# Layer 1's feature products scaled on ScalarE, comparisons for four groups at once, and another order of the first transfers, in a four-layer graph network

## The chip, the cores and the metric

The kernel runs on one core of a Trainium2 chip. A core has five engines that run their own instruction streams in order: TensorE (PE; weight loads are shown apart as PEld) multiplies matrices into PSUM, VectorE (DVE) and ScalarE (ACT) work elementwise, GpSimd (POOL) here mostly issues indirect transfers (gathers and scatters by index), and SyncE (SP) issues plain transfers. ScalarE issues some transfers as well. The metric is the device time of one launch in microseconds: the median over runs, here 4229.58 us (3 runs, 4228.15 to 4233.15).

## The reference

3125 nodes with 256 features each, 50000 edges sorted by their destination, 16 edge types, 64 features per edge. Four layers, each a graph part and a mixture or feed-forward part. Only the first half of the computation matters here, layers 0 and 1:

```python
# layer 0, graph part: a matrix for each of 16 edge types
transformed = jnp.einsum('ni,rio->rno', layernorm(x), weight)
x = x + segment_sum(transformed[rel_type, src] * norm, dst)
# layer 0, mixture of 8 experts, two of them per node
x = x + moe(layernorm(x))
# layer 1, graph part: messages from an embedding table, weighted by edge features
cut = 0.5 * (cos(edge_weight * pi / CUTOFF) + 1.0) * (edge_weight < CUTOFF)
W = (edge_feats @ W_dist + b_dist) * cut[:, None]
agg = segment_sum(embed_table[node_z][src] * W, dst)
x = x + concatenate([layernorm(x), agg], 1) @ W_comb + b_comb
```

The output is x after four such layers. Everything is float32.

## The kernel before

One stage computes both layers' graph parts and layer 0's experts together (`stage_one`, L787). Ahead of it, from L378 on, the edges' fields are loaded as 125 x 400 arrays and written to DRAM as rows of a table `md` (source, type code, norm, destination, cut). x is loaded in five pieces of five node tiles each (`xs0`, L408). From each node's statistics DVE and ScalarE make the normalized rows; POOL gathers the embedding row of each node (`species`, L453); both halves together are a row of 512 numbers, and five writes (L633) put the 3150 rows into a DRAM table `tab`. A search finds where each node's edges begin: POOL fetches a row of destinations from the DRAM array `dsr` (L573), and DVE counts in it (L578). `dsr` is written by SP (L542, L543). The start of the program also has a branch for unsorted edges, which each engine passes before it comes to L541. The order of all instructions in this part and in the stage is written out by hand for each engine.

The nodes are cut into 25 tiles of 126, a tile into 21 groups of 6 nodes. The edges that end in one group lie in a window of 128 places; there are 521 windows. For a window:

- POOL gathers the 128 source rows from `tab` (`fetch_rows`, nine buffers `g`), and SP loads the transposed edge features (`fetch_feats`, six buffers `f`).
- `build` (L855), two windows ahead, makes two comparison matrices on DVE: `s0`, 128 x 96, is 1 where the edge has this node and type, times norm (L865), and `s1`, 128 x 32 (or 128 x 128 for the groups 5 and 10, which straddle two quarters of the rows), is 1 where the edge has this node, times the cut (L867).
- `window` (L873): PE multiplies the rows' normalized half with `s0` into the PSUM tile `c` (L880), which ScalarE copies to `aT` (L884), for two windows at once where they are neighbours. PE multiplies the features with `W_dist` into `pw` (L887, two PSUM banks). DVE multiplies `pw` with the rows' embedding half into `mt` (L890). After this the row buffer is free, and the gather of the window nine places on is issued.
- `add_up` (L895) multiplies `s1` with `mt` into the tile's sum `agg` in PSUM (L906), in three batches of windows.

After a tile's windows come eight slots of `weigh` (L914): 64 matmuls of `aT` with the 16 type matrices `wrel` into `f0` (L919). After the last of them DVE adds `f0` to x (L923). Each pair of tiles then starts a `Flow`: routing, experts and combination, cut into 22, 32 and 34 steps, which are laid between later windows (`between`, L1139). `between` runs once after each window and each `weigh` slot: it takes the due steps of the flows, one step of `background` (in every slot up to slot 116, then in every third), one of `late_weights` (weights on ScalarE's DMA queue) and one of `first_zeros` (zero fills of DRAM on SP's queue, 200 KB each).

`background` (L1195) prepares later layers: the searches for the other tiles, a check of windows, a product of all edge features with an attention vector (`b_at`, L1273 to L1284: 100 loads of 125 KB, two buffers, each used one step after it is issued), and a ranking of nodes by degree (L1347), where for each of 25 columns three products are accumulated: a row `base`, the columns before (`prev`) and this column.

After the last tile the remaining flow steps run one after the other. Then the stage's memory is given back, and the other layers follow, which the change does not touch.

Of the kernel before, what the change touches and what calls it, by code (L numbers as in the profile page):

```python
# [19 lines left out]
P = 128  # L20
# [75 lines left out]
def tile_gnn_ffn(ctx: ExitStack, tc: tile.TileContext, a: dict, out: bass.AP):  # L96
# [311 lines left out]
    for i in range(5):  # L408
        xg = pp.tile([P, 5, D], F32, name=f"n_x{i}")
        t = 5 * i  # L410
        m = 5 if i < 4 else 4
        if i == 4:
            nc.gpsimd.memset(xg[:, 4, :], 0.0)
            nc.sync.dma_start(xg[:TV, 4, :], a["x"][(NT - 1) * TN :, :])
        nc.sync.dma_start(xg[:TN, :m], a["x"][t * TN : (t + m) * TN, :].rearrange("(t p) d -> p t d", p=TN))
        xs0.append(xg)
        if i == 0:
            wgt = edge_in("edge_weight", F32)
            norm = edge_in("edge_weight1", F32)
# [122 lines left out]
    nc.sync.dma_start(dsr[1:, :], dstf)  # L542
    nc.sync.dma_start(dsr[:1, :], none)  # L543
# [55 lines left out]
    nc.sync.dma_start(md[:, E:].rearrange("f (p c) -> p f c", c=P), pads)  # L599

# [186 lines left out]
    def stage_one(late, cp, eb):  # L787
# [36 lines left out]
        def quarter(j):  # L824
            return None if j in (5, 10) else GN * j // 32
# [29 lines left out]
        def build():  # L855
            k = nxt["s"]
            if k < len(wins):
# [4 lines left out]
                a = quarter(j)  # L862
                a, m1 = (0, P) if a is None else (32 * a, 32)
                s1 = eb.tile([P, m1], F32, name=f"s1_{m1}", bufs=13 if m1 == 32 else 3)
                nc.vector.tensor_scalar(s0, iota_f[:, :GW], m[:, F_CODE, j : j + 1], m[:, F_NORM, j : j + 1],  # L865
                                        op0=OP.is_equal, op1=OP.mult)
                nc.vector.tensor_scalar(s1, iota_f[:, a : a + m1], m[:, F_DST, j : j + 1], m[:, F_CUT, j : j + 1],  # L867
                                        op0=OP.is_equal, op1=OP.mult)
                sums[k] = s0, s1
# [3 lines left out]
        def window(k):  # L873
# [5 lines left out]
            for h in range(2):  # L879
                nc.tensor.matmul(pc[:, h, o : o + GW], g[:, h * P : (h + 1) * P], sums[k][0], start=True, stop=True)  # L880
# [8 lines left out]
            mt = mults[t, j] = eb.tile([P, D], F32, name="mt", bufs=11), sums.pop(k)[1]  # L889
            nc.vector.tensor_tensor(mt[0], pw, rows.pop(k)[:, D:], op=OP.mult)  # L890
            fetch_rows()

        ag_of, mults = {}, {}

        def add_up(t, b):  # L895
# [4 lines left out]
            for js in together[b]:  # L900
                js = [j for j in js if (t, j) in mults]
                for j in js:
                    a = quarter(j)
                    mt, s1 = mults.pop((t, j))
                    o = agg if a is None else agg[32 * a : 32 * a + 32]
                    nc.tensor.matmul(o, s1, mt, start=not begun, stop=(j == 10), skip_group_check=True)  # L906
# [7 lines left out]
        def weigh(t, i):  # L914
# [224 lines left out]
        def between(fast=False):  # L1139
# [7 lines left out]
            next(loads, None)  # L1147
            next(zeros_, None)
# [3 lines left out]
        for _ in range(2):  # L1152
            build()
# [5 lines left out]
        for t in range(NT):  # L1159
            n = GL if t == NT - 1 else GC  # L1160
            for j in range(n):
                build()
                window(k)
                k += 1

# [15 lines left out]
            for i in range(8):  # L1181
# [3 lines left out]
                if i == 7 and (t % 2 or t == NT - 1):  # L1185
                    if t == NT - 1:
                        load_e(t // 2, 0)
                    flows.append(Flow(t // 2))
# [6 lines left out]
    def background(eb, bank):  # L1195
# [77 lines left out]
        for b in range(0, ET, AB):  # L1273
            at = eb.tile([EP, AB, 64], F32, name="b_at", bufs=2)
            nc.sync.dma_start(at, attr[:, b : b + AB, :])
            if b:
                old, b0 = prev
                nc.vector.tensor_tensor(old, old, a3[:EP].unsqueeze(1).to_broadcast([EP, AB, 64]), op=OP.mult)
                nc.vector.tensor_reduce(rect[:, b0 : b0 + AB, 1], old, axis=AX.X, op=OP.add)
            prev = at, b  # L1280
            yield
        old, b0 = prev
        nc.vector.tensor_tensor(old, old, a3[:EP].unsqueeze(1).to_broadcast([EP, AB, 64]), op=OP.mult)
        nc.vector.tensor_reduce(rect[:, b0 : b0 + AB, 1], old, axis=AX.X, op=OP.add)  # L1284
# [1256 lines left out]
```

## Time and profile before

| | |
|---|---|
| median of 3 runs | 4229.58 us |
| the profiled execution | 4229.5 us, span 4227.7 us |
| first window's matmul (L880) | 90.38 us after the span's start |
| last `weigh` matmul of the first tile | 164.4 us |
| of the last tile | 1762.6 us |
| last store of the stage issued (L1106) | 1864.6 us |
| DVE: product `mt` (L890) | 521 of 420 ns |
| DVE: comparison `s0` (L865), `s1` (L867) | 341 ns; 308 ns (32 wide), 347 ns (128 wide) |
| ScalarE: copies of `c` (L884) | 875 ns (two windows), 517 ns (one) |
| PE: products `pw` (L887) | 1042 of 445 ns |

An instruction on PE counts twice for float32: a matrix product is shown as two matmuls, each with its weight load. Matmuls overlap, so their durations do not add up to time. In the views, "idle before" or the brackets behind a line give the time that the engine stood idle before the instruction, and what ended it. Of the rest of the span, 1865 to 4228 us, nothing reads or writes what the change touches.

### The profile page before, as it was taken

The page shows a single profiled execution, that of the slowest core. Times are in us where ns is not written, and L with a number is a line of the kernel's source. Part 1 is how long each engine was busy: PE and PEld are TensorE (multiplying, and loading weights), DVE is VectorE, ACT ScalarE, POOL GpSimd, SP SyncE. Part 2 cuts the span into 40 slices and gives each one's busy share as a digit, 9 for nine tenths or more (in the row PEclk, how much of TensorE's full clock was granted, in tenths as well). Part 3 has the DMA queues.
Part 4 walks back from the last instruction along what each step waited for, and adds up shares of the span by engine and source line. Part 5 has one row for each costly group of instructions (what it writes and reads, how often), then busy time and mean ns, then how long its engine had stood idle before and what let it go on. Part 6 is the DMA issues. An engine that isn't in the chain of part 4 may idle for free. (4 is left out here: it accounts for less than half of the span.)

```text
span 4227.7 us, 46661 instructions
## 1 busy us (share of the span) xinstructions
PE 2697.7 (64%) x12940; PEld 2134.4 (50%) x12940; DVE 1946.6 (46%) x7501; ACT 845.3 (20%) x1803; POOL 1758.5 (42%) x1996
## 2 busy tenths in 40 slices
PE   1688999989889999948411365365670112137875
PEld 0566878767677878737310254254550111125653
DVE  3445666665665555442344333444662233245300
ACT  1112232221122222211100021122220000013322
POOL 4342333341253333002466544544437666643323
PEclk9878999999799999968755576577775555566987
DMA  7766455452243444113233254365523333323543
GB/s 223 223 190 187 129 157 144 130 154 65 76 118 107 118 133 126 52 48 107 73 93 91 86 175 141 107 185 168 174 90 101 87 92 88 92 81 107 158 159 100
DMA packets 275971, 521.46 MB, mean 123 GB/s; under 512 B 53609, under 2 KB 176897, under 8 KB 275685
## 3 DMA queue, kind: packets, MB, share of 16 engines
q0 software_dynamic: 105344, 306.57, 25.0%
q1 hardware_dynamic: 159598, 201.27, 15.6%
q10 hardware_dynamic: 10742, 10.34, 0.8%
q8 instruction: 114, 1.87, 0.2%
q14 instruction: 173, 1.41, 0.1%
HBM read 431.19 MB, written 86.78 MB: 123 GB/s over the span
## 5 line engine op out<-in xcount | busy, mean ns | idle before, releaser
L136 POOL DMA_INDIRECT g<-tab,m_si x521 | 498.0, 956 | 989.9 <-DVE mt L890 526.5
L136 POOL DMA_INDIRECT g_rows<-tab,srcI x413 | 401.9, 973 | 300.4 <-DVE ACC L2273 157.3
L136 POOL DMA_INDIRECT g_row<-tab,srcI x413 | 400.4, 970 | 196.3 <-issue 104.6
L880 PEld LDWEIGHTS c<-s,g 128*128 128x128 f32 x2084 | 345.8, 217 | 166.7 <-issue 83.9
L880 PE MATMUL c<-s,g 128*128 128x96 f32 x2084 | 356.1, 299 | 100.1 <-issue 38.2
L887 PE MATMUL pw<-w_d,f 65*128 65x256 f32 x1042 | 374.4, 445 | 14.2 <-DVE mt L890 11.9
L919 PE MATMUL f<-w_rel,aT 128*126 128x256 f32 x1600 | 372.6, 383 | 0.1
L884 ACT COPY aT<-c 128x384 f32<-128x384 f32 (+1 forms) x323 | 237.1, 737 | 595.7 <-PE c L880 397.5
L1982 PE MATMUL mm<-ro_xt,ro_w 128*128 128x192 f32 (+3 forms) x928 | 255.9, 428 | 122.3 <-ACT ro_h L2063 73.1
L919 PEld LDWEIGHTS f<-w_rel,aT 128*126 128x126 f32 x1600 | 300.2, 190 | 50.5 <-issue 5.3
L1651 PE MATMUL tp<-ident,ACC 128*128 128x128 f32 x50 | 16.1, 424 | 462.5 <-DVE ACC L2395 357.2
L890 DVE TENSOR_TENSOR mt<-pw,g 128x256 f32<-128x256 f32 x521 | 218.7, 420 | 159.0 <-PE pw L887 83.8
L1986 PE MATMUL y<-ro_w,ro_h 128*96 128x256 f32 (+2 forms) x1040 | 263.6, 409 | 33.5 <-ACT ro_h L2063 19.1
L1982 PEld LDWEIGHTS mm<-ro_xt,ro_w 128*128 128x128 f32 x928 | 183.8, 221 | 178.4 <-ACT ro_h L2063 80.5
L1651 PEld LDWEIGHTS tp<-ident,ACC 128*128 128x128 f32 x50 | 7.1, 199 | 470.5 <-issue 441.1
L1986 PEld LDWEIGHTS y<-ro_w,ro_h 128*96 128x96 f32 (+2 forms) x1040 | 190.4, 189 | 86.9 <-ACT ro_h L2063 23.1
L1037 PE MATMUL w<-w,b_h 128*126 128x256 f32 x800 | 218.5, 398 | 11.1 <-ACT xt L950 3.0
L1028 PE MATMUL w<-xt,w 128*128 128x252 f32 (+1 forms) x832 | 221.3, 392 | 6.3 <-issue 3.4
L140 POOL DMA_INDIRECT xg<-XX,ro_pos x100 | 101.6, 1016 | 287.6 <-issue 136.5
L2273 DVE SCALAR_TENSOR_TENSOR ACC<-g_rows,g_e,ACC 128x256 f32<-128x256 f32 x413 | 200.9, 486 | 43.9 <-DVE ACC L2273 19.9
L2395 DVE TENSOR_TENSOR ACC<-ACC,g_row 128x256 f32<-128x256 f32 x413 | 173.2, 424 | 67.1 <-DMA g_row<-tab,srcI 48.0
L2240 PE MATMUL pu<-w_s,a_xt 128*128 128x256 f32 x100 | 45.9, 606 | 231.5 <-DVE ACC L2268 104.8
(580 smaller groups left out, 4791.0 us busy)
## 6 DMA issues: line engine op xcount, KB each, us to landing
ro_w<-in_L_ffn_blocks SPq DMA_DIRECT2D x58, 514.0 KB
ro_w<-in_L_ffn_blocks SPq DMA_DIRECT2D x58, 512.0 KB
f<-in_attr_t SPq DMA_DIRECT2D x521, 32.5 KB
xg<-zero SPq DMA_DIRECT2D x78, 200.0 KB
b_at<-in_edge_attr SPq DMA_DIRECT2D x100, 125.0 KB
tabr<-v SPq DMA_DIRECT2D x12, 758.0 KB
g<-tab,m_si POOLq DMA_INDIRECT x521
g_rows<-in_L_ffn_blocks SPq DMA_DIRECT2D x14, 514.0 KB
```

Source lines behind the costliest of these rows:

```text
L136: return nc.gpsimd.indirect_dma_start(out=dst, out_offset=None, in_=table, in_offset=bass.IndirectOffsetOnAxis(ap=idx, axis=0))
L880: nc.tensor.matmul(pc[:, h, o : o + GW], g[:, h * P : (h + 1) * P], sums[k][0], start=True, stop=True)
L884: nc.scalar.copy(aT[:, :, :, b : b + n * GN].rearrange("p k r n -> p k n r"), pc[:, :, : n * GW].rearrange("p k (n r) -> p k n r", r=16))
L887: nc.tensor.matmul(pw, feats.pop(k), wd, start=True, stop=True)
L890: nc.vector.tensor_tensor(mt[0], pw, rows.pop(k)[:, D:], op=OP.mult)
L919: nc.tensor.matmul(cur["f"][:TN], aT[:, h, r, :], wrel[:, h, r, :], start=(r == 0 and h == 0), stop=(r == 15 and h == 1))
L1028: nc.tensor.matmul(ph, w["01"][:, e, k, i * P : (i + 1) * P], xt[:, k, : n * TN], start=(k == 0), stop=(k == 1))
L1037: nc.tensor.matmul(py, last[:, k, i * TN : (i + 1) * TN], w["02"][:, e - 1, k, :], start=(k == 0), stop=(k == 1))
L1982: nc.tensor.matmul(ph, w[:, o : o + P], xt[:, k, :], start=(k == 0), stop=(k == 1))
L1986: nc.tensor.matmul(py, h[:, i, s], w[:, i * D : (i + 1) * D], start=(i == 0), stop=(i == self.fc - 1))
L2273: stt(u, g[:, r, :D], e[:, r0 + r : r0 + r + 1], u, op0=OP.mult, op1=OP.add)
L2395: nc.vector.tensor_tensor(u, u, rows.pop(r), op=OP.max)
```

## The change

1. The factor `cut` moves. Before, `s1` was the comparison times `cut`. Now ScalarE reads `pw` from PSUM, multiplies by the edge's `cut` and writes `mt`, and DVE multiplies `mt` by the gathered embedding half in place.
2. The comparisons `s1` leave `build`. `whose` makes them once per batch: for the batches 0 and 1 one comparison has four groups (`s1g`, 128 x 4 x 32), two per batch; for batch 2 five single ones, without a second operation.
3. `build` runs three windows ahead instead of two.
4. The addition of `f0` to x and the start of the pair's flow move from the last `weigh` slot to the second window of the next tile (`weighed`); the last tile keeps its place.
5. Of x's five loads the first two stay at the beginning, the other three are issued by SP after the `md` writes. The two writes of `dsr` go from SP's queue to ScalarE's.
6. `late_weights` begins at slot 2 and `first_zeros` at slot 6, instead of slot 0.
7. `b_at` has three buffers and is used two steps after its issue.
8. In the ranking the row `base` is put into row 0 of `prev` once, and the separate product of one row goes.

```diff
     xs0 = []
-    for i in range(5):
+
+    def load_x0(i):
...
-        if i == 0:
-            wgt = edge_in("edge_weight", F32)
-            norm = edge_in("edge_weight1", F32)
+
+    load_x0(0)
+    wgt = edge_in("edge_weight", F32)
+    norm = edge_in("edge_weight1", F32)
+    load_x0(1)
...
-    nc.sync.dma_start(dsr[1:, :], dstf)
-    nc.sync.dma_start(dsr[:1, :], none)
+    nc.scalar.dma_start(dsr[1:, :], dstf)
+    nc.scalar.dma_start(dsr[:1, :], none)
...
     nc.sync.dma_start(md[:, E:].rearrange("f (p c) -> p f c", c=P), pads)
+    for i in range(2, 5):
+        load_x0(i)
...
-                a = quarter(j)
-                a, m1 = (0, P) if a is None else (32 * a, 32)
-                s1 = eb.tile([P, m1], F32, name=f"s1_{m1}", bufs=13 if m1 == 32 else 3)
                 nc.vector.tensor_scalar(s0, iota_f[:, :GW], m[:, F_CODE, j : j + 1], m[:, F_NORM, j : j + 1],
                                         op0=OP.is_equal, op1=OP.mult)
-                nc.vector.tensor_scalar(s1, iota_f[:, a : a + m1], m[:, F_DST, j : j + 1], m[:, F_CUT, j : j + 1],
-                                        op0=OP.is_equal, op1=OP.mult)
-                sums[k] = s0, s1
+                sums[k] = s0
...
-            mt = mults[t, j] = eb.tile([P, D], F32, name="mt", bufs=11), sums.pop(k)[1]
-            nc.vector.tensor_tensor(mt[0], pw, rows.pop(k)[:, D:], op=OP.mult)
+            del sums[k]
+            mt = mults[t, j] = eb.tile([P, D], F32, name="mt", bufs=11)
+            nc.scalar.activation(mt, pw, AF.Copy, scale=mts[t][:, F_CUT, j : j + 1])
+            nc.vector.tensor_tensor(mt, mt, rows.pop(k)[:, D:], op=OP.mult)
             fetch_rows()
...
+        def whose(t, b):
+
+            m = mts[t][:, F_DST]
+            n = GL if t == NT - 1 else GC
+            for js in together[b]:
+                js = [j for j in js if j < n]
+                if b < 2:
+                    s1 = eb.tile([P, 4, 32], F32, name="s1g", bufs=3)
+                    of = m[:, js[0] : js[-1] + 1 : 5].unsqueeze(2).to_broadcast([P, len(js), 32])
+                    nc.vector.tensor_tensor(s1[:, : len(js)], iota_f.rearrange("p (q n) -> p q n", n=32)[:, : len(js)],
+                                            of, op=OP.is_equal)
+                    for i, j in enumerate(js):
+                        ones_of[t, j] = s1[:, i, :]
+                    continue
+                for j in js:
+                    q = quarter(j)
+                    n1 = P if q is None else 32
+                    s1 = ones_of[t, j] = eb.tile([P, n1], F32, name=f"s1_{n1}", bufs=2 if q is None else 3)
+                    o = 32 * (q or 0)
+                    nc.vector.tensor_scalar(s1, iota_f[:, o : o + n1], m[:, j : j + 1], None, op0=OP.is_equal)
...
-            if i == 7:
-                x = x_of[t // 2][:TN, t % 2, :]
-                nc.vector.tensor_add(x, x, cur["f"][:TN])
+
+        def weighed(t):
+            x = x_of[t // 2][:TN, t % 2, :]
+            nc.vector.tensor_add(x, x, cur["f"][:TN])
+            if t % 2 or t == NT - 1:
+                flows.append(Flow(t // 2))
...
-            next(loads, None)
-            next(zeros_, None)
+            if slot >= 2:
+                next(loads, None)
+            if slot >= 6:
+                next(zeros_, None)
...
-        for _ in range(2):
+        for _ in range(3):
             build()
...
                 build()
+                at = wins[k][1]
+                if at in (12, 13, 5):
+                    whose(t, (12, 13, 5).index(at))
                 window(k)
                 k += 1
+                if j == 1 and t:
+                    weighed(t - 1)
...
-        for b in range(0, ET, AB):
-            at = eb.tile([EP, AB, 64], F32, name="b_at", bufs=2)
-            nc.sync.dma_start(at, attr[:, b : b + AB, :])
-            if b:
-                old, b0 = prev
+        ahead = []
+        for b in range(0, ET + 2 * AB, AB):
+            if b < ET:
+                at = eb.tile([EP, AB, 64], F32, name="b_at", bufs=3)
+                nc.sync.dma_start(at, attr[:, b : b + AB, :])
+                ahead.append((at, b))
+            if b >= 2 * AB:
+                old, b0 = ahead.pop(0)
...
+        nc.vector.tensor_copy(prev[:1, :], base[:1, :])
...
-            nc.tensor.matmul(pk, ones[:1, :], base[:1, :], start=True, stop=False)
-            nc.tensor.matmul(pk, ones, prev, start=False, stop=False)
+            nc.tensor.matmul(pk, ones, prev, start=True, stop=False)
```

More of the change, by code (lines that the diff above doesn't have):

```diff
@@ L879, in window @@
             for h in range(2):
-                nc.tensor.matmul(pc[:, h, o : o + GW], g[:, h * P : (h + 1) * P], sums[k][0], start=True, stop=True)
+                nc.tensor.matmul(pc[:, h, o : o + GW], g[:, h * P : (h + 1) * P], sums[k], start=True, stop=True)
             if second[k] or k + 1 == len(wins) or not second[k + 1]:
@@ L888, in window @@
             fetch_feats()
-            mt = mults[t, j] = eb.tile([P, D], F32, name="mt", bufs=11), sums.pop(k)[1]
-            nc.vector.tensor_tensor(mt[0], pw, rows.pop(k)[:, D:], op=OP.mult)
+            del sums[k]
+            mt = mults[t, j] = eb.tile([P, D], F32, name="mt", bufs=11)
+            nc.scalar.activation(mt, pw, AF.Copy, scale=mts[t][:, F_CUT, j : j + 1])
+            nc.vector.tensor_tensor(mt, mt, rows.pop(k)[:, D:], op=OP.mult)
             fetch_rows()
-        ag_of, mults = {}, {}
+        ag_of, mults, ones_of = {}, {}, {}
+        def whose(t, b):
[17 more added lines that the diff above has]
+                    nc.vector.tensor_scalar(s1, iota_f[:, o : o + n1], m[:, j : j + 1], None, op0=OP.is_equal)
         def add_up(t, b):
@@ L903, in add_up @@
                     a = quarter(j)
-                    mt, s1 = mults.pop((t, j))
                     o = agg if a is None else agg[32 * a : 32 * a + 32]
-                    nc.tensor.matmul(o, s1, mt, start=not begun, stop=(j == 10), skip_group_check=True)
+                    nc.tensor.matmul(o, ones_of.pop((t, j)), mults.pop((t, j)), start=not begun, stop=(j == 10),
+                                     skip_group_check=True)
                 begun = True
@@ L1184, in stage_one @@
                     add_up(t, 2)
[L1185 to L1188, printed above, removed]
+                if i == 7 and t == NT - 1:
+                    load_e(t // 2, 0)
+                    weighed(t)
                 between()
@@ L1272, in background @@
         nc.vector.tensor_copy(rect[:, :, 0], srcf)
-        for b in range(0, ET, AB):
-            at = eb.tile([EP, AB, 64], F32, name="b_at", bufs=2)
-            nc.sync.dma_start(at, attr[:, b : b + AB, :])
-            if b:
-                old, b0 = prev
+        ahead = []
[6 more added lines that the diff above has]
+                old, b0 = ahead.pop(0)
                 nc.vector.tensor_tensor(old, old, a3[:EP].unsqueeze(1).to_broadcast([EP, AB, 64]), op=OP.mult)
                 nc.vector.tensor_reduce(rect[:, b0 : b0 + AB, 1], old, axis=AX.X, op=OP.add)
-            prev = at, b
             yield
-        old, b0 = prev
-        nc.vector.tensor_tensor(old, old, a3[:EP].unsqueeze(1).to_broadcast([EP, AB, 64]), op=OP.mult)
-        nc.vector.tensor_reduce(rect[:, b0 : b0 + AB, 1], old, axis=AX.X, op=OP.add)
         nc.vector.tensor_sub(ews, ews, rect[:, :, 1])
```

## The prediction

> **What bounds the kernel now.** I read the page first: TensorE has the most work, and the digits by slice show where it is dense.
>
> ```profile
> PE 2697.7 (64%) x12940; PEld 2134.4 (50%) x12940; DVE 1946.6 (46%) x7501; ACT 845.3 (20%) x1803; POOL 1758.5 (42%) x1996
> PE   1688999989889999948411365365670112137875
> PEclk9878999999799999968755576577775555566987
> DMA  7766455452243444113233254365523333323543
> ```
>
> Each slice is 105.7 us. The change touches only layer 1's stage (slices 1 to 18); its last store is issued at 1864.6. So I cut that stage with the table by stretches, at the ends of the node tiles' last `weigh` matmuls. Columns: stretch, busy time of PE, PEld, DVE, ACT, POOL, then clock, DMA share, GB/s.
>
> ```profile
> 0.00:90.00 90.00, 2.36 (x7) 1.47 (x7) 29.72 (x135) 13.28 (x23) 34.99 (x54) 1.00 0.67 206
> 90.00:164.00 74.00, 57.23 (x236) 44.37 (x237) 32.65 (x146) 9.93 (x14) 30.16 (x32) 1.00 0.87 279
> 250.00:317.00 67.00, 60.74 (x268) 48.22 (x268) 38.05 (x152) 15.81 (x24) 25.56 (x27) 0.69 0.63 189
> 317.00:400.00 83.00, 68.06 (x309) 53.98 (x308) 45.07 (x137) 14.18 (x23) 20.82 (x22) 0.81 0.62 194
> 464.00:523.00 59.00, 57.01 (x322) 48.15 (x321) 35.54 (x129) 16.45 (x29) 21.24 (x22) 0.97 0.46 131
> 1291.00:1763.00 472.00, 451.27 (x2550) 374.53 (x2548) 250.53 (x1030) 134.67 (x250) 157.91 (x190) 0.98 0.41 115
> ```
>
> Three regimes. Up to 90 us nothing runs on PE: transfers and their order bound it. The first tile (74 us) runs at a DMA share of 0.87. A later tile takes 59 us with PE busy 97%: there PE is the bound. Between them tile 3 takes 83 us, PE 82% busy at 0.81 clock. What its DVE and PE wait for is told by the waits and the timeline:
>
> ```profile
> DVE b_at L1278 <- DMA b_at<-in_edge_attr: 36.1, 27, 3.1
> PE c L880 <- issue: 26.5, 22, 5.3
> PE c L880 <- DVE s L865: 21.8, 16, 4.1
> PE pw L887 <- DVE mt L890: 7.9, 9, 1.4
> ```
>
> (The first is of 317 to 400, the others of 317 to 1763.) And the pieces of the timeline that carry the start:
>
> ```profile
> 35.23 0.32 SPq L542 DMA_DIRECT2D dsr<-e_dstf  x1
> 39.76 0.91 POOL L136 DMA_INDIRECT q_rows<-dsr,q_rowi  x1 [16.33 <-DMA dsr<-e_dstf]
> 46.98 0.62 DVE L578 TENSOR_SCALAR_CACHE_REDUCE q_rows<-q_rows,q_node 21x400 f32<-21x400 f32 x1 [12.52 <-DMA q_rows<-dsr,q_rowi]
> 84.57 0.18 DVE L798 TENSOR_SCALAR j<-iota_f 128x21 f32<-128x21 f32 x1 [24.39 <-DMA tab<-n_row]
> ```
>
> SP issues `dsr` at 35.23 although DVE had it at 19.94: five loads of x (issued up to 26.25) and then the start's branch stand before it on SP. POOL then loses 16.33 us and DVE 12.52 us, and the table is only written at 84.5.
>
> **The change, part by part.** The sum is against the profiled 4229.5 us (span 4227.7 and 1.8 around); the median of the runs is 4229.58.
>
> *A, the start: -18 us.* Three x loads (1.9 MB) move behind SP's `md` writes, and `dsr` goes to ScalarE's queue, free at about 20 us. POOL's 16.33 us and DVE's 12.52 us go, as both were waiting for `dsr`. What is late next: statistics of tiles 10 to 14 are interleaved with the first reciprocal roots, and their x now lands after some 1 MB of writes, perhaps 3 us late; then the table. POOL's embedding gathers ended at 66.3 and would end at about 50 to 57; the table's last write then lands at 64 to 69 instead of 84.5. DMA allows it: from 30 to 45 us it moved 32 to 126 GB/s. Also the first 2 MB of `w_rel`, issued at 58.24 between the table's writes, move out to slot 2: 2.1 MB at 350 GB/s are 6 us, inside the 18. Ends: -25 (all waits and `w_rel`), -5 (x is late and only `w_rel` counts).
>
> *B, the first tile: +5 us.* That `w_rel` lands here, less six zero fills of 0.2 MB: 0.9 MB at the stretch's 279 GB/s is 3 us. ScalarE's queue is in order: the small loads behind `w_rel` held it from 93.4 to 109.8 (the `aT` copy waited 15.59 us). Now `mt` of each window stands behind them too, with the gathers that wait for it and, after two PSUM banks, PE. Ends: 0 (the DMA is full anyway) and +14 (that wait once more).
>
> *C, tiles 1 to 4: -25 us.* `b_at` gets a third buffer and is used two steps after its issue. DVE stood 51.5 us for it between 150 and 423 us; a transfer issued at 317.05 was used at 318.94, 1.9 us later, and a slot of that tile takes 2.4 or more, so two steps cover it. Behind those waits stood the x addition and `build`; PE ran dry (at 407.6 for 5.3 us, at 325.2 for 4.1) and its clock fell. Tile 3 at 62 instead of 83 gives 21, tile 4's start 5, tile 2 about 0: I take 25. Ends: -51 and 0 (the transfers are late by more under a DMA share of 0.62).
>
> *D, the later tiles: -20 us.* DVE loses 21 comparisons per tile (308 ns, two of 347) and gets 4 grouped ones (nearest row: 128x128 addition, 293 ns) and 5 single ones: 6.5 - 2.7 = 3.8 us per tile, 95 in all. It is busy 53 to 60%, so I count this only where PE waited for DVE. `mt` keeps its 420 ns; from SBUF a 128x256 product took 424. `build` runs three ahead instead of two, and the x addition no longer stands before it. Of the rows above, 56 us, some 17 are already in C; of the remaining 39 I take half. The half-rate clock that follows each such stall costs up to 70 us from 464 to 1763 (stretch times one less the clock), so the end is -80 with part of it; the other end is +36: ScalarE adds 521 products. Their row is missing; the nearest are a PSUM copy of 126x256 (372 ns) and a scaled SBUF activation (590); I take 0.42, near the copy, which also reads PSUM: 219 us on an engine busy 28% in the dense stretch. The cover is PE: of a 59 us tile 19 go to eight `weigh` slots and 40 to 21 window slots, 1.9 us each, in which ScalarE needs 0.46 for `aT` (237 us over 521), 0.42, and some 0.4 for the flows. Behind the new wait stand `aT` copies and `b_h` on ScalarE, and on DVE, after `mt`, the flows' additions; POOL's gathers run nine windows ahead and bear 1 us. If a sixth of the 0.42 reaches PE in each window, that is 0.07 x 521 = +36.
>
> The rule against this part is in the Trainium skill, ScalarE: Activation LUTs, Rules for kernel authors: products belong on VectorE rather than ScalarE. The trace says ScalarE is 20% busy and DVE 46%, so I don't follow it. By the rule, part D would bring nothing and the sum would be 20 us less gain.
>
> *E, the rank loop: -7 us.* 25 products of one row go (50 passes, 345 ns each, overlapped). In the timeline a step takes 1.06 us at full clock, of which they hold 0.42, and 0.72 at half clock; DVE itself needs 0.95 per step. So 25 x 0.1 to 25 x 0.72: 2.5 to 18. One 1-row copy is added: nothing.
>
> *F, the tail: +2 us.* A flow now starts two slots later. Covered while windows run; the last pair's two steps fall in the tail, 102 us for 88 steps. Ends 0, +4.
>
> Zero fills six slots later, and loads two, cost nothing elsewhere: 317 to 400 has DMA at 0.62, and the first `weigh` is at slot 21.
>
> One rule speaks against A: the Trainium skill, DMA: Bandwidth & Descriptors, Issuing engines are not separate DMA queues, says that another issuing engine saves only the sequencer's issue time. By it, moving `dsr` would save its two issues, 0.5 us, and A would be the 6 us of `w_rel`. The row at 35.23 is a case in which the issue itself waits, so I keep -18.
>
> Sum: -18 + 5 - 25 - 20 - 7 + 2 = -63: 4229.5 - 63 = 4166.5, say **4166 us**.
>
> **The rivals.**
> 1. *The clock recovers too.* Most half-rate time goes with the stalls: C -40, D -55, others as above: 4229.5 - 18 + 5 - 40 - 55 - 7 + 2 = 4116. For it: clock 0.69 in 250 to 317 without a long gap. Against it: searches that wait for DMA in tiles 1 and 2 stay.
> 2. *Only the start gains.* PE's gaps are filled by other waits (gathers, PSUM banks): A + B + E with its lower end + F = -18 + 5 - 2.5 + 2 = -13.5: 4216. For it: PE is already 96% busy from 1291. Against it: 36.1 us of one wait in one tile.
> 3. *ScalarE becomes the wait (slower).* Each window's `mt` stands behind an `aT` copy (875 ns per pair) and PE waits for the PSUM bank of `pw`. From 63/521 = 0.12 us of PE per window on, the gain is gone; at half of the 0.42 it costs 0.21 x 521 = 109 us in place of D's -20: -63 + 20 + 109 = +66, 4296. Against it: ScalarE waited 304 us for `c`, so it is early nearly everywhere.
> 4. *The order of transfers does nothing* (table bound by bytes): A = -6: 4178, inside the likeliest one's range.
>
> **How the numbers follow.** Likeliest, with rival 4, 60%: 4130 to 4205. Rival 1 15%. Rival 2 14%, of which 4% lies within 0.2%. Rival 3, 8%; 3% for a small loss by B and D's bad ends together. 0.2% is 8.5 us, about what a measurement of this kernel can tell from no change. Faster 0.86, same 0.04, slower 0.10. For the range I leave out the far half of rival 1 and what is slower: 4100 to 4224.
>
> **What would show it.** A: the first `c` matmul at about 72 instead of 90.4, `dsr` issued near 20. B: the first tile at 74 to 85 us. C: no `b_at` wait on DVE above 10 us in all, tile 3 near 62. D: PE's wait for `s` and for the bank of `pw` together under 20 us from 317; the scaled copies at 0.37 to 0.47. E: a rank step under 1.0 us. F: last `weigh` to last store about 104. Wrong would be: PE waiting for ScalarE in the hundreds of windows, gathers late by it, or a start still held by x or the table.

## The result: 1.05% slower where 1.5% faster was forecast

The changed kernel took 4278.0 us (median of 4 runs, 4269.8 to 4279.4), the kernel before 4231.4 us beside it: ratio 1.0105, 95% interval 1.0088 to 1.0123. The forecast was 4166 us with a range to 4224, and faster with a chance of 0.86. It was wrong in sign.

The same kernel before the change took 4216 to 4240 us in the first and the last of six sessions and 3744 to 3768 us in the four between (below: the slower and the quicker sessions), so that times are compared within a session, and across sessions only as ratios to the kernel before. The change was measured in one of each: slower by 1.05% in the first, and a gain, 0.9943 (0.9927 to 0.9959), in a quicker one. The record gives the chip number 15 to the fourth session, a quicker one, and to the last, a slower one. The texts of expectation below, written before that was known, say "the first chip" and "the later chips" for slower and quicker.

The profile after the change, of the slower kind (its execution 4278.99 us, span 4277.3). First the page's totals and slices:

```profile
PE 2702.8 (63%) x12890; PEld 2142.7 (50%) x12890; DVE 1882.7 (44%) x7205; ACT 1039.4 (24%) x2324; POOL 1768.8 (41%) x1996
...
PE   1689999988888999966612364456671112137975
...
PEclk9669999989889999987855576577775555556987
```

DVE lost 64 us of work and ScalarE got 194 us more, as the change says. PE's digits in the stage went from 9 to 8 in places: it has the same work and more gaps. Next the same stretches as before (columns as before: stretch, PE, PEld, DVE, ACT, POOL, clock, DMA share, GB/s):

```profile
0.00:90.00 90.00, 10.32 (x35) 8.51 (x35) 32.65 (x149) 15.11 (x26) 41.38 (x60) 1.00 0.64 204
90.00:164.00 74.00, 48.94 (x204) 38.31 (x204) 26.97 (x119) 16.93 (x32) 24.07 (x26) 0.77 0.87 273
317.00:400.00 83.00, 76.55 (x391) 61.59 (x389) 51.45 (x154) 28.67 (x56) 24.10 (x26) 0.92 0.69 219
1291.00:1763.00 472.00, 437.04 (x2396) 363.07 (x2395) 219.80 (x890) 177.98 (x381) 160.47 (x190) 0.95 0.39 110
```

The start is earlier (35 matmuls of PE before 90 us instead of 7), 317 to 400 does 391 matmuls instead of 309 at a clock of 0.92 instead of 0.81, and 1291 to 1763, where PE was the bound, does 2396 instead of 2550. The loss is in the late part. Cut at the ends of the tiles' `weigh` matmuls, in us of one profiled execution each, and with the forecast's terms:

| part | forecast | slower session | quicker session |
|---|---|---|---|
| A: first `c` matmul | -18 | 90.4 to 82.0: -8.3 | 89.3 to 83.4: -5.9 |
| B: from there to the first tile's end | +5 | +9.4 | +0.8 |
| C: tiles 1 to 4 | -25 | -12.5 | -16.7 |
| D and E: tiles 5 to 24 | -27 | 1299.1 to 1357.8: +58.7 | 1234.8 to 1226.2: -8.6 |
| F: from the last `weigh` matmul to the end of the span | +2 | +2.3 | +1.8 |
| sum (spans) | -63 | +49.6 | -28.6 |

So one line of the table is the error of sign: in the slower session D and E have 86 us more than forecast. What PE waited for in it, before (first fence, 463.5 to 1762.6 us) and after (second fence, 452.1 to 1809.9 us; columns: total, times, longest):

```profile
PE c L880 <- DVE s L865: 15.6, 13, 3.8
PE c L880 <- issue: 15.5, 17, 3.0
PE pw L887 <- DVE mt L890: 7.6, 8, 1.4
...
PE w L1037 <- ACT xt L950: 2.7, 5, 0.6
...
PE w L949 <- ACT xt L950: 1.9, 1, 1.9
...
PE w L1351 <- DVE k_prev L1353: 1.5, 2, 1.2
```

```profile
PE w L975 <- ACT xt L976: 19.1, 6, 6.0
PE pw L887 <- ACT mt L891: 15.0, 9, 3.0
PE pw L887 <- issue: 11.3, 6, 5.4
PE w L1382 <- DVE k_prev L1384: 10.8, 13, 3.1
...
PE w L975 <- issue: 7.1, 5, 4.1
...
PE c L880 <- DVE s L867: 5.5, 9, 1.4
```

The waits that the change was to remove did go: the rows of `c` (L880), 36.3 us with the small ones, fell to 17.5. In their place came the PSUM bank of `pw`, now released by ScalarE (26.3 us in place of 9.9), and the flows' transposes (`flip_rows`, L975; L949 before), 35.8 us in place of 2.2. All rows that name ScalarE together grew from 9.9 to 55.6 us, +45.7; PE's idle time in all grew from 82.2 to 127.4, +45.2. The time at half clock grew from 133 to 191 us. In the quicker session the same rows show almost nothing of it (changed kernel, 438.2 to 1664.4 us):

```profile
PE w L1054 <- ACT xt L976: 5.1, 10, 0.5
PE w L975 <- ACT b_h L1056: 1.5, 4, 0.4
```

There the rows that name ScalarE grew from 6.5 to 9.9 us only. PE's idle time in all rose there too, from 46.6 to 57.2 us, but the time at half clock fell from 92 to 68 us.

What differs between the sessions is seen in one flow's two transposes. The timeline of the changed kernel in the slower session, tile 23:

```profile
1709.89 0.43 PE L975 MATMUL w<-ident,xn 126*128 126x126 f32 x2
...
1711.04 0.26 PE L809 MATMUL w<-ident,m_m 105*128 105x105 f32 x1
1714.20 0.37 ACT L976 COPY xt<-w 128x252 f32<-128x252 f32 x1 [4.17 <-remote]
...
1714.62 0.43 PE L975 MATMUL w<-ident,xn 126*128 126x126 f32 x2 [3.33 <-ACT xt L976]
```

and the same instructions in the quicker session:

```profile
1573.21 0.43 PE L975 MATMUL w<-ident,xn 126*128 126x126 f32 x2
...
1573.68 0.37 ACT L976 COPY xt<-w 128x252 f32<-128x252 f32 x1 [0.61 <-PE w L975]
...
1574.37 0.26 PE L809 MATMUL w<-ident,m_m 105*128 105x105 f32 x1
...
1574.46 0.38 PE L975 MATMUL w<-ident,xn 126*128 126x126 f32 x2
```

In the quicker session ScalarE copies as soon as the transposes end, at 1573.64. In the slower one PE's records show the transposes done at 1710.3, and ScalarE, idle, starts at 1714.20, released by nothing that the profile names. The trace's semaphore events (the signals by which one engine releases another) show it: of PE's completions none is recorded from 1708.97 to 1714.07, and then seven within 0.24 us, as many as PE's instructions of that stretch signal. PE's signals came late, in a burst. Counted as a silence of over 1.5 us followed by three signals within 0.2 us, there are 33 such bursts (116 us of silence) in tiles 5 to 24 of the kernel before and 15 (72 us) in the changed one, in the slower session; in the quicker sessions' traces there is none, whatever the kernel. In the slower traces 14 to 16% of PE's signal records are missing and 23 to 25% of VectorE's, so the counts are rough; VectorE's signals, counted in the same way, show one such burst before and none after. The changed kernel lost more although it met fewer bursts, so their number does not explain its loss.

### The profile page after: what moved, and what is told of

It is laid out like the page before. It is cut to its first block, busy times and chain, and to the rows that moved or that the text cites. A ratio compares the mean times of both kernels' runs of the same rounds, so it can differ in the third digit from the quotient of the medians.

```text
span 4277.3 us, 46755 instructions
## 1 busy us (share of the span) xinstructions
PE 2702.8 (63%) x12890; PEld 2142.7 (50%) x12890; DVE 1882.7 (44%) x7205; ACT 1039.4 (24%) x2324; POOL 1768.8 (41%) x1996
## 5 line engine op out<-in xcount | busy, mean ns | idle before, releaser
L880 PEld LDWEIGHTS c<-s,g 128*128 128x128 f32 x2084 | 353.9, 220 | 100.2 <-issue 39.8
L892 DVE TENSOR_TENSOR mt<-mt,g 128x256 f32<-128x256 f32 x521 | 220.0, 422 | 405.1 <-ACT mt L891 346.6
L880 PE MATMUL c<-s,g 128*128 128x96 f32 x2084 | 356.7, 300 | 45.4 <-DMA f<-in_attr_t 21.5
L942 PE MATMUL f<-w_rel,aT 128*126 128x256 f32 x1600 | 382.5, 390 | 2.9 <-ACT aT L884 1.9
L891 ACT ACTIVATE mt<-pw,m_mt 128x256 f32<-128x256 f32 x521 | 245.6, 473 | 374.5 <-PE pw L887 232.7
L1682 PE MATMUL tp<-ident,ACC 128*128 128x128 f32 x50 | 16.3, 428 | 464.6 <-DVE ACC L2426 446.3
L1054 PE MATMUL w<-xt,w 128*128 128x252 f32 (+1 forms) x832 | 224.9, 396 | 10.5 <-ACT xt L976 6.6
L2017 PEld LDWEIGHTS y<-ro_w,ro_h 128*96 128x96 f32 (+2 forms) x1040 | 190.5, 189 | 81.4 <-issue 26.6
L1063 PE MATMUL w<-w,b_h 128*126 128x256 f32 x800 | 221.9, 404 | 7.9 <-ACT xt L976 5.3
L887 PEld LDWEIGHTS pw<-w_d,f 65*128 65x128 f32 x1042 | 183.2, 219 | 43.3 <-ACT mt L891 29.7
```

The costliest lines, as they stand in the source:

```text
L887: nc.tensor.matmul(pw, feats.pop(k), wd, start=True, stop=True)
L891: nc.scalar.activation(mt, pw, AF.Copy, scale=mts[t][:, F_CUT, j : j + 1])
L892: nc.vector.tensor_tensor(mt, mt, rows.pop(k)[:, D:], op=OP.mult)
L942: nc.tensor.matmul(cur["f"][:TN], aT[:, h, r, :], wrel[:, h, r, :], start=(r == 0 and h == 0), stop=(r == 15 and h == 1))
L1054: nc.tensor.matmul(ph, w["01"][:, e, k, i * P : (i + 1) * P], xt[:, k, : n * TN], start=(k == 0), stop=(k == 1))
L1063: nc.tensor.matmul(py, last[:, k, i * TN : (i + 1) * TN], w["02"][:, e - 1, k, :], start=(k == 0), stop=(k == 1))
```

## The experiments

**The ScalarE step.** Two edits: the changed kernel with the product and the cut in one VectorE instruction, and the kernel before with the ScalarE step alone.

```diff
-            nc.scalar.activation(mt, pw, AF.Copy, scale=mts[t][:, F_CUT, j : j + 1])
-            nc.vector.tensor_tensor(mt, mt, rows.pop(k)[:, D:], op=OP.mult)
+            stt(mt, pw, mts[t][:, F_CUT, j : j + 1], rows.pop(k)[:, D:], op0=OP.mult, op1=OP.mult)
```

```diff
-                nc.vector.tensor_scalar(s1, iota_f[:, a : a + m1], m[:, F_DST, j : j + 1], m[:, F_CUT, j : j + 1],
-                                        op0=OP.is_equal, op1=OP.mult)
+                nc.vector.tensor_scalar(s1, iota_f[:, a : a + m1], m[:, F_DST, j : j + 1], None, op0=OP.is_equal)
...
-            nc.vector.tensor_tensor(mt[0], pw, rows.pop(k)[:, D:], op=OP.mult)
+            nc.scalar.activation(mt[0], pw, AF.Copy, scale=mts[t][:, F_CUT, j : j + 1])
+            nc.vector.tensor_tensor(mt[0], mt[0], rows.pop(k)[:, D:], op=OP.mult)
```

> The changed kernel, but ScalarE no longer takes part in the product: VectorE makes pw times cut times the gathered half in one instruction. All else as changed. Theory 1 (the ScalarE step is what costs): of the 58.7 us that the tiles 5 to 24 lost, at least 45 come back, the last weigh matmul ends at 1750 to 1765 us instead of 1809.9, time 4215 to 4235. Theory 2 (the later start of the flows is what costs, because their steps now fall on other slots): less than 15 us come back, time 4262 to 4280.

> The kernel before with one part of the change alone: s1 is the bare comparison, ScalarE multiplies pw by the cut from PSUM, VectorE multiplies by the gathered half in place. Comparisons stay single and in their place. Theory 1: slower by 45 to 85 us than before (4275 to 4315): the loss of the tiles 5 to 24, plus what it does in the first five. Theory 2: within 15 us of before, 4220 to 4245.

> Once more the changed kernel with the product on VectorE alone, in the hope of a chip like the first one (before: about 4230 us). There: theory 1 (on that chip the completion signals of TensorE reach the other engines late, in bursts, and with the ScalarE step in the chain these pauses come back to TensorE): ratio 0.985 to 0.993, tiles 5 to 24 as long as before (1299 us) or shorter. Theory 2 (the loss there comes from the late flows or the other parts): ratio 1.004 to 1.012. On a chip like the later ones (3754 us): 0.988 again.

> Once more the kernel before with the ScalarE step alone. On a chip like the first: theory 1: 50 to 80 us slower than before (ratio 1.012 to 1.019). Theory 2: as on the later chips, ratio 1.004.

All four ran in quicker sessions (before: 3754 and 3756 us). Without the step: 3711.9 us, ratio 0.9881 (0.9851 to 0.9910), and again 3719.0 us, 0.9899 (0.9878 to 0.9919). The step alone: 1.0040 (1.0026 to 1.0054), and again 1.0038 (1.0025 to 1.0051), about 15 us slower. Against the changed kernel's 0.9943 the step's removal is worth 17 and 23 us, each uncertain by 10 us or more by its intervals. The traces, one of each run, show where. From the first `c` matmul to tile 4's end the step alone takes 379.7 and 379.2 us, the kernel before 370.7; tiles 5 to 24 take 1244.6 and 1243.9 against 1234.8. The changed kernel takes 354.8 and 1226.2 us for the two parts, without the step 345.7 and 346.4, and 1220.2 and 1218.9. So the step costs about 9 us in the first tiles and 6 to 10 in the later ones. That the step alone shows only 15 us is due to the start: there its `mt` of the first window delays the load of `w_rel`, and the table is ready earlier (see A below). The step does not cost the 47 us of the first result there, and the absolute times in these expectations, drawn for 4230 us, cannot be met.

**The later flows.** The changed kernel with the x addition and the flow's start in the last `weigh` slot again, and both undoings together.

```diff
-                if j == 1 and t:
-                    weighed(t - 1)
...
-                if i == 7 and t == NT - 1:
-                    load_e(t // 2, 0)
+                if i == 7:
+                    if t == NT - 1:
+                        load_e(t // 2, 0)
                     weighed(t)
```

> The changed kernel, but the addition of f0 to x and the start of the pair's flow stand in the last weigh slot again, as before. The ScalarE step stays. Theory 1 (the ScalarE step costs): within 12 us of the changed kernel, 4266 to 4290. Theory 2 (the flows' shift by two slots costs): at least 40 of the 58.7 us come back, time 4225 to 4240, and the odd tiles (5, 7, 9, 11, 15, 17, 19, 21, 23) are as long as before the change.

> The two undoings of the runs before it together: VectorE makes the product with the cut in one instruction, and the flows start in the last weigh slot. What stays of the change is the grouped comparison, the comparisons three windows ahead, the third b_at buffer, the order of the first transfers and the shorter rank step. If the costs of the two parts are independent, its gain over the changed kernel is the sum of the gains of the two. Theory 1 and theory 2 both: 4195 to 4225, as the 11.4 us gained up to tile 4 stay and the tail is as before; the last weigh matmul ends at 1735 to 1755.

> Once more the changed kernel with the flows started in the last weigh slot. On a chip like the first: theory 1 (the ScalarE step): ratio 1.004 to 1.012, as for the whole change. Theory 2 (the late flows): ratio 0.988 to 0.996. On a chip like the later ones: 0.992 again.

Quicker sessions: 0.9920 (0.9894 to 0.9947) and 0.9939 (0.9921 to 0.9957) with the flows early, against 0.9943 for the whole change; 0.9892 (0.9864 to 0.9919) with both undone, against 0.9881 and 0.9899 with the step alone undone. The flows' place shows no gain or loss there beyond the intervals. Between the two runs of one session that differ in the step alone (3728.9 and 3714.4 us) it again costs 14.5 us.

**Both kernels again, in a quicker session.** No edit.

> The changed kernel once more, on the chip of the other runs, whose times are some 11% shorter (3754 us before the change). With the ScalarE step and the early flows the first runs gave 0.992 here, without the step 0.988. Theory 1 (the ScalarE step alone costs, the same 14 us here with either place of the flows, since the runs without it are 14.5 us shorter when the flows are early): 3715 to 3735, ratio 0.990 to 0.995; the change is then a gain here, and the loss belongs to the first chip. Theory 2 (the step and the late flows together cost): 3765 to 3800, ratio 1.003 to 1.012, as on the first chip.

> The kernel before, for its trace on this chip. Theory 1 (the chips differ in what all engines do, for example by pauses): its tiles from 5 on end earlier than on the first chip by about as much per us as the later stages do, which are 17% shorter here. Theory 2 (the chips differ only in the later stages): tiles 5 to 24 take the same 1299 us as on the first chip. 3754 us.

The changed kernel: 3733.3 us, 0.9943; theory 1's range held. The kernel before: 3757.1 us; its tiles 5 to 24 took 1234.8 us, not 1299: 5% less, where the later stages took 16% less, so neither of its two theories holds as written. Of the 472 us between its two traces 68 lie before the last `weigh` matmul and 404 in the later stages, which the change does not touch. So the loss was seen only where signals are late, in the one such session that measured the change, and what the change does there had to be read from the traces.

**The third `b_at` buffer.** The first undoing, with the old two buffers:

```diff
-                at = eb.tile([EP, AB, 64], F32, name="b_at", bufs=3)
+            at = eb.tile([EP, AB, 64], F32, name="b_at", bufs=2)
...
+            if b:
+                old, b0 = prev
```

> The changed kernel with the product on VectorE alone (as in the first of these runs), and the b_at loads as before the change: two buffers, each used one step after its issue. Theory 1 (the third buffer brings what part C said, -25 us in tiles 2 to 4): 20 to 30 us longer than the run with three buffers, tile 3 at 76 to 85 us instead of 66, about 3735 here. Theory 2 (tile 3 is shorter for another reason, fewer comparisons or the earlier ones): within 8 us of it, tile 3 below 70.

3737.6 us, 0.9953 (0.9937 to 0.9970), against 3718.9 us, 0.9898, for the next experiment's first kernel in the same session, which kept three (its other edit brought nothing): 18.7 us, just under theory 1's 20 to 30. Tile 3 took 76.8 us, with three buffers 66 to 69. DVE's wait from 160 to 1700 us, with two buffers and with three:

```profile
DVE b_at L1309 <- DMA b_at<-in_edge_attr: 57.1, 42, 5.3
```

```profile
DVE b_at L1313 <- DMA b_at<-in_edge_attr: 34.0, 26, 4.9
```

Part C is right in cause, and three quarters of its size. Three buffers do not end the wait: a transfer used two steps after its issue is still late 26 times.

**The start.** Without the ScalarE step, once with the fill of the last x piece ahead on GpSimd, once with all five x loads at the beginning:

```diff
+    x4 = pp.tile([P, 5, D], F32, name="n_x4")
+    nc.gpsimd.memset(x4[:, 4, :], 0.0)
     load_x0(0)
```

```diff
-    load_x0(1)
+    for i in range(1, 5):
+        load_x0(i)
...
-    for i in range(2, 5):
-        load_x0(i)
```

> The changed kernel with the product on VectorE alone, and the fill of the last x piece's padding put first on GpSimd instead of behind ten embedding gathers; all loads keep their order. Theory 1 (the start gains too little because the last x piece is issued only after that fill, 12 us late, and the gather of the edge table and ten more embedding gathers wait for its statistics): the first c matmul at 68 to 75 us instead of 81.5, first tile's end 6 to 10 us earlier, time 4 to 10 us shorter than without. Theory 2 (x in its new place lands late anyway, or the table's writes are the limit): the first c matmul within 3 us of 81.5, time the same.

> The changed kernel with the product on VectorE alone, and all five x loads at the beginning again; dsr stays on ScalarE's queue. Theory 1 (the start gained 8 us and not 18 because three x pieces now land late, and GpSimd waits for their statistics until 51 us): norms at 34 us instead of 43, the edge table's gather at 40 to 46 instead of 51, first c matmul at 72 to 77 instead of 81.5, 4 to 9 us shorter than with the product on VectorE alone. Theory 2 (the writes of the edge table, which now stand behind the x loads again, or the bandwidth, hold it): the first c matmul at 80 or later, same time or longer.

Theory 2 held both times. First `c` matmul at 84.4 and 86.1 us, where the same kernel without either edit had 81.5 and 86.0 in its two runs; ratios 0.9898 (0.9878 to 0.9918) and 0.9888 (0.9871 to 0.9906). GpSimd's waits show the reason. The changed kernel, in order of time:

```profile
23.22 0.53 ACTq L545 DMA_DIRECT2D dsr<-e_dstf  x1
...
28.18 3.41 SPq L416 DMA_DIRECT2D n_x<-in_x  x2
...
28.75 0.92 POOL L136 DMA_INDIRECT q_rows<-dsr,q_rowi  x1 [5.79 <-DVE n_st L621]
...
44.05 5.03 ACT L636 ACTIVATE n_row<-n_x,n_nm,rs_r 126x256 f32<-126x256 f32 x10 [16.17 <-DVE n_nm L628]
51.46 0.98 POOL L136 DMA_INDIRECT m_m<-md,mixI  x1 [11.10 <-DVE n_st L621]
```

What VectorE's statistics wait for stands in the same trace:

```profile
39.24 0.43 DVE L621 BATCH_NORM_STATS2 n_st<-n_x 126x6 f32<-126x256 f32 x1 [9.94 <-DMA n_x<-in_x]
```

The fill first, and x first:

```profile
54.71 0.97 POOL L136 DMA_INDIRECT m_m<-md,mixI  x1 [13.58 <-DVE n_st L622]
```

```profile
37.07 0.92 POOL L136 DMA_INDIRECT q_rows<-dsr,q_rowi  x1 [13.88 <-DVE e_cu L667]
...
49.92 0.97 POOL L136 DMA_INDIRECT m_m<-md,mixI  x1 [1.58 <-DVE n_st L620]
```

`dsr` is written 12 us earlier, and GpSimd's 16.33 us for it are gone; but it now waits 5.79 + 11.10 = 16.89 us for x's statistics, which stand ahead on DVE for x that lands later. Bring x forward, and the 13.88 come back at the search. In every order, that of the kernel before included, the edge table's gather is issued at 50 to 55 us and the last write of `tab` at 69 to 73.

What did gain at the start can be read from the run of the step alone, which keeps the old order of the transfers but delays one. The first half of `w_rel` (2 MB), issued before the change while `tab` is written, stands there behind the first window's `mt` on ScalarE. Before, and with the step alone:

```profile
58.24 0.41 ACTq L696 DMA_DIRECT2D w_rel<-in_L_gnn_weight  x1
```

```profile
79.30 0.18 DVE L798 TENSOR_SCALAR j<-iota_f 128x21 f32<-128x21 f32 x1 [20.21 <-DMA tab<-n_row]
...
87.26 0.45 ACTq L696 DMA_DIRECT2D w_rel<-in_L_gnn_weight  x1
```

VectorE's wait for `tab` ends at 79.3 and, in the second run, 77.2 us, where three traces of the old order have 83.6 to 86.3, and the first `c` matmul comes at 85.0 and 83.0 us instead of 89.3 to 92.0. The kernels with the new order have it at 81.5 to 86.1. So the place of this one load accounts for most of what the start gained.

**Pauses at windows 5 and 15.** If the step or the late flows make every late signal dear, so should pauses that hold ScalarE and VectorE (26 small copies and one long sum, whose results nothing uses).

```diff
+        def hold():
+            for _ in range(26):
+                nc.scalar.copy(idle[:, 0], iota_f[:, :8])
+            nc.vector.tensor_reduce(idle[:, 1, :1], wrel[:, 0].rearrange("p r d -> p (r d)")[:, :3600], axis=AX.X, op=OP.add)
...
+                if j in (5, 15) and t >= 5:
+                    hold()
```

> The kernel before, with ScalarE and VectorE each kept busy by idle work for about 4 us after the windows 5 and 15 of the tiles 5 to 24 (ScalarE: 26 copies of 8 columns; VectorE: one sum over 3600 columns), 40 times in all, about as often and as long as TensorE's completion signals came late on the first chip. TensorE, GpSimd and the transfers are not held. Theory 1 (the kernel before rides over such a pause better than the changed one, because VectorE alone stands between TensorE's product and its PSUM bank): this kernel loses less than the changed one does, per pause 0.5 to 2 us: 20 to 80 us here. Theory 2 (both ride alike): the loss here and that of the changed kernel lie within 15 us.

> The changed kernel with the same 40 pauses. Theory 1: its loss against the changed kernel without pauses (ratio 0.994 to the kernel before, 3735 us) is at least 40 us greater than that of the kernel before with pauses against the one without (3756). Theory 2: the two losses agree within 15 us.

> The changed kernel with the product on VectorE alone and the same 40 pauses. Theory 1 (the ScalarE step is what makes the pauses dear): its loss against the same kernel without pauses (0.989, 3715 us) is no greater than that of the kernel before, within 15 us. Theory 3 (the late flows make them dear): its loss is that of the changed kernel, within 15 us.

> The changed kernel with the flows started in the last weigh slot, and the same 40 pauses. Theory 1: its loss against the same kernel without pauses (0.993, 3730 us) is that of the changed kernel, within 15 us. Theory 3: it is that of the kernel before, within 15 us.

A quicker session (before: 3757.6 us). In the traces a pause was 5.9 us on ScalarE and 3.9 us on VectorE.

| kernel | without | with 40 pauses | loss |
|---|---|---|---|
| before | 1 | 1.0555 (1.0528 to 1.0583) | 5.55%, 209 us |
| changed | 0.9943 | 1.0405 (1.0374 to 1.0435) | 4.62%, 174 us |
| changed, without the ScalarE step | 0.9881, 0.9899 | 1.0350 (1.0323 to 1.0377) | 4.51 to 4.69%, 169 to 176 us |
| changed, flows early | 0.9920, 0.9939 | 1.0568 (1.0541 to 1.0595) | 6.29 to 6.48%, 236 to 243 us |

Each loss is far above the 20 to 80 us that were expected for the kernel before. Theory 1 falls: the changed kernel bears these pauses better than the one before, and the step makes no difference to them. Theory 2, equal losses, falls with it (209 and 174 us). Theory 3 falls too: late flows made them cheaper. Pauses of this kind at these two places are not the mechanism.

**A pause between a flow's two transposes.** The trace points at a narrower place. Ten gaps of over 0.8 us stand before a `flip_rows` transpose in tiles 5 to 24 of the changed kernel in the slower session, and eight of them, 26.6 us, stand right behind L809, the transpose of the next tile's edge table at window 10. All the stage's small products share two PSUM banks; where the table's transpose comes between the two transposes of a flow's rows, the second has to wait for ScalarE's copy of the first. In the changed kernel L809 stands directly ahead of such a transpose in 19 tiles, in the kernel before in 9 and with no gap: the flows start two slots later. Two runs put 20 pauses between the first transpose and its copy, and the second moves the table:

```diff
+                if j == 9 and t >= 5:
+                    hold()
```

```diff
-META_AT = 10
+META_AT = 8
```

> The changed kernel with one pause per tile (tiles 5 to 24, 20 in all) of the kind of the runs before it, laid after window 9: between the first transpose of a flow's rows and its copy on ScalarE, where the first chip's late signals cost most (eight gaps of TensorE before a second transpose that stands right behind the next tile's edge-table transpose). Theory A (in the changed kernel these three products come within one slot and share two PSUM banks, so the second transpose of the rows waits for the copy of the first, and TensorE has one window of slack): TensorE waits for that copy in most tiles, 2 to 4 us each; together with the run with the table at slot 8 this one is 25 to 80 us longer. Theory B (banks don't matter, a pause costs the same there as at any place): the two lie within 10 us.

> The run before it with one number changed: the next tile's edge-table transposes at window 8 instead of 10, so that the two transposes of a flow's rows have the two banks to themselves. The same 20 pauses. Theory A: no wait of TensorE for the first copy, 25 to 80 us shorter than the run before it. Theory B: within 10 us of it.

They fell into a slower session (before: 4228.4 us), so real late signals came on top. 4366.7 us, 1.0346 (1.0305 to 1.0388), and with the table at window 8 4352.0 us, 1.0290 (1.0246 to 1.0335). PE's waits from 452 to 1900 us, first with the table at 10, then at 8:

```profile
PE w L975 <- ACT xt L976: 60.5, 11, 8.6
PE w L975 <- ACT b_h L1056: 56.3, 9, 7.6
PE pw L887 <- ACT mt L891: 15.6, 7, 7.5
```

```profile
PE w L1054 <- ACT xt L976: 51.8, 10, 8.2
PE w L1063 <- ACT b_h L1056: 38.2, 9, 5.2
...
PE pw L887 <- ACT mt L891: 7.8, 4, 2.6
```

With the table at 10 each of the 19 second transposes behind L809 waits, 4.1 to 8.6 us. With the table at 8 these two rows, 116.8 us, fall to 2.3, so it is the table's transpose between the two, on the shared banks, that makes the second wait. But 90.0 us, where these products had 7.5 for ScalarE, are in the next products that need ScalarE's copy or one of the two banks (L1054, L1063), and the gain is 14.7 us, with intervals that overlap, between the 10 us that theory B allowed and the 25 that theory A asked for. Theory A is right about the wait and wrong about its worth: the table's place moves the wait more than it takes it away.

## Why the prediction was wrong, step by step

**A (-18).** Failed at "what is late next". The text gave x's later landing "perhaps 3 us"; it is 16.9 us of waits of GpSimd for x's statistics, in place of the 16.33 removed. What remained, -8.3 and -5.9 us, is near the 6 us that the text counted for `w_rel` moving out of the table's way: rival 4, and the step alone, which delays `w_rel` and moves nothing else at the start, has 4 to 7 of it.

The rule of the Trainium skill that I set aside (DMA: Bandwidth & Descriptors, Issuing engines are not separate DMA queues) had the better sum here. The issue did wait, and `dsr` was written 12 us earlier, but the next wait on GpSimd took its place.

**B (+5).** +9.4 and +0.8: inside its ends, 0 and +14.

**C (-25).** Mechanism right, size -19 by the two-buffer run, in tiles 3 and 4 as said. The claim that no wait above 10 us would remain was wrong: 30.5 us in 24 waits remained in the slower session from 160 to 1840 us.

**D (-20).** The step that gave the wrong sign. Three things in it hold: the scaled copy took 0.473 us, against 0.42 taken; PE's waits at `c` fell by half; and without the ScalarE step the tiles 5 to 24 gained 14.6 us in a quicker session (1234.8 to 1220.2), E included, about half of the 27 forecast for D and E. Two fail. The ScalarE step was costed at nothing, "the cover is PE", and costs 6 to 10 us in these tiles where signals come at once, and some 9 more in the first tiles, where the text had no term for it but B's upper end; the +36 of the text covers that, but was not taken. The rule of the Trainium skill that I did not follow (ScalarE: Activation LUTs, Rules for kernel authors: products to VectorE) gave the better answer, although ScalarE is busy 28% of the span in the quicker sessions and the instructions are near each other, 473 ns for the scaled copy and 420 for VectorE's product. Why the step costs time there is not shown. That it adds a link to the chain from PE to VectorE and stands in ScalarE's queue behind copies is the likely reason, but in tiles 5 to 24 PE's rows that name ScalarE are 9.8 us with it and 6.5 without, and PE's idle time 57.2 and 59.1.

And in the slower session PE waited 45.7 us more for ScalarE, and 58 us more ran at half clock. This is the step that failed: D and F let PE's work cover whatever ScalarE adds, and with late signals it did not. It is rival 3's wait, with a part that the text did not see: the flows' shift was costed in the tail alone (F), and in the windows it put the second transpose of a flow behind the edge table's transpose in every tile, on two shared banks. That the trace shows: eight gaps, 26.6 us, beside 45.2 us more idle time in all. The signals' lateness was there to be read in the trace before, as waits put down to "issue" or "remote" and as PE's completions in bursts; I counted only who had waited, not what slack was left.

**E (-7).** From the first step's start to the last step's end, windows between included, -3.4 us in the slower session (85.4 to 82.0) and -4.7 in the quicker (82.1 to 77.4). Most steps take 0.84 to 0.93 instead of 1.06 us, as said, but PE then waits for DVE's `prev`: 10.8 us in all, 1.5 before.

**F (+2).** +2.3 and +1.8 to the end of the span, but only +0.4 and +1.2 of it up to the last store. Its cost inside the windows, put at nothing, is what D's account above shows.

The listed chances add to 0.85 for faster and 0.11 for slower, not 0.86 and 0.10; nothing hangs on it.

What stays open: how much of the 58.7 us is due to the ScalarE step and how much to the flows' place when signals are late. By PE's rows of waits the bank of `pw` has 16.4 us more, the flows' transposes 33.6 more and `c` 18.8 less, but a wait is not a change of time. The kernels with one of them undone ran in quicker sessions only, and the artificial pauses are not the real ones: at windows 5 and 15 they spoke against both. The evidence for the place is the gaps of the two traces and the pair at window 9, which shows the wait and a gain that its intervals do not secure. Why PE's signals are late in some sessions is open as well; it is not the change, as the kernel before has them, and not the chip alone, if the number 15 stands for one chip.

The version without the ScalarE step beats both kernels in the quicker sessions: 0.9881 and 0.9899, against 0.9943 for the change. In a slower session it was not measured.

## What to carry to other kernels

A low busy share does not make work on an engine free: here 521 products cost 15 us and more with ScalarE 28% busy, and the form that makes the product in one VectorE instruction was the faster one. Look at what else the move delays on that engine; a load that it issues can come later, for better or worse. When steps move by some slots, list what else uses the same PSUM banks in their new slots, not only what they do at the end of the stage. A wait that is removed is worth what the next wait on the same engine leaves of it: GpSimd's 16.3 us for one transfer became 16.9 us for another.

## What the runs showed of the hardware that I had not expected

One program has two levels of time, 4228 and 3756 us, in two sessions with the same chip number, without any difference in the work. In the slower traces PE's completions reach the other engines in bursts after silences of 1.5 to 11 us in this stage, while PE's own records run on; in the quicker ones never. In the later stages PE, ScalarE and SyncE stand for longer: in the kernel before PE's last products end at 2423.4 us, and ScalarE and SyncE, both waiting for PE's signals, resumed together at 2439.01. Late signals and missing records of signals come in the same traces (in the quicker ones under 0.4% of PE's, VectorE's and ScalarE's are missing); whether the recording has a part in the lateness these runs can't tell. And a small pause was not absorbed by queues that look idle: 5.9 us on ScalarE and 3.9 us on VectorE cost 4.2 to 6.1 us of time each.
